# Sums of exponentials of two attention units folded to 64 partitions by DMA, with one product of ones for both

## The chip, the cores and the metric

The kernel runs on one core of one Trainium2 chip. The metric is the device time of that core in microseconds; before the change it is 3346.09 us, the median of three runs (3346.06 to 3346.24). In texts and profile lines PE is TensorE (PEld its weight loads), DVE is VectorE, ACT is ScalarE, POOL is GpSimd and SP is SyncE.

## What is computed

The reference is a chain of four layers on an image of two batches, 512 channels and 32 x 32 positions, all in float32. Layer 0 is a deformable attention with a learned position bias and an MLP, layer 1 a linear attention. Layers 2 and 3, which the change touches, are the same kind of layer: group norm, queries, keys and values for 8 heads of 64 channels, softmax attention over 1024 positions, a projection and the residual. Cut to what matters (layer 2):

```python
attn = jnp.einsum('bhcn,bhcm->bhnm', q, k) * scale
attn = jax.nn.softmax(attn, axis=-1)
out = jnp.einsum('bhnm,bhcm->bhcn', attn, v)
```

## The kernel before, in words

In layers 2 and 3 the method `attention` computes queries, keys and values, and then, where the logits are small enough for exponentials without a maximum, `heads_bounded` does the attention. Only that method is changed.

`heads_bounded` works through 16 units, one after the other. A unit is a batch b, a pair of heads p (two heads of 64 channels fill 128 partitions), and a half h of the 1024 queries (512 of them). Each unit has eight steps n, one for each block of 128 keys. In a step:

- `score` (L1509) forms the logits of both heads for these 128 keys: four products of 64 x 64 weights, one in each quadrant of TensorE, into a PSUM place of 128 x 1024. Two places, "a" and "b", take turns from step to step. ScalarE makes the exponentials e from it (L1513). So the score of a step needs the place that the exponential of two steps before has read.
- The exponentials of the eight steps are added up: those of steps 0, 1, 3, 5 on GpSimd in the tile `some` (L1518, L1520), those of 2, 4, 6, 7 on VectorE in the tile `sum` (L1523, L1525), and the two at the end of the unit (L1527). The tile `some` has a single buffer.
- `value` (L1538), two steps behind, multiplies the exponentials with the values, again in four quadrants; the result o collects over eight steps in the PSUM place "even" (h = 0) or "odd" (h = 1). The keys of one block lie on two halves of the partitions, and each half has its own sum in o: at the end ScalarE copies one (L1547) and VectorE adds the other (L1548).

Then the result has to be divided by the sums of exponentials. `divide` (L1550 on) multiplies `sum` with a matrix of ones, which adds over 64 partitions and spreads the sum over 64 rows at once: four products in four quadrants (L1555), into d in the PSUM place that o has just left. The two halves of the partitions give two partial sums: ScalarE copies the one (L1559), VectorE adds the other (L1560), takes the reciprocal (L1561) and multiplies the result with it (L1563). The bias of the values is put into a list and later added by ScalarE (L1567).

The order on TensorE, ScalarE, VectorE and GpSimd is written out by hand: within `manual_schedule` the instructions stand on each engine in the order in which the loop over i (128 steps and two more) issues them. In step i come `score(i)` with its exponential and additions, then, where i is a multiple of 8, a waiting bias, then `value(i - 2)`, then, where i % 8 is 4, `divide` of the unit before. From i = 78 on, every eighth step (i % 8 = 6) puts two additions for the projection on GpSimd (L1577, L812 on). The last unit's `divide` stands in the projection that follows. No scheduler moves any of it; semaphores are all that makes an engine wait.

Of the kernel before, what the change touches and what calls it, by code (L numbers as in the profile page):

```python
# [11 lines left out]
F32 = mybir.dt.float32  # L12
AF = mybir.ActivationFunctionType
ALU = mybir.AluOpType
# [4 lines left out]
P = 128  # L19
# [35 lines left out]
class Net:  # L55
# [1419 lines left out]
    def heads_bounded(self, k, ones, data, proj, out):  # L1475
# [7 lines left out]
        with ExitStack() as ctx:  # L1483
# [9 lines left out]
            def place(x, name):  # L1493
                return places[x].tile([P, 2, HF], F32, tag="o", name=name)
# [4 lines left out]
            def score(unit, n):  # L1499
                b, p, h, state = unit  # L1500
                qs, ks, _ = data[b]
                cut = slice(h * HF, (h + 1) * HF)

                at = {0: "b", 1: "a", 2: "odd"}.get(n) if unit is units[0] else None
                s = place(at or ("a", "b")[n % 2], f"s{k}{b}{p}{h}{n}")
                for par, rows in enumerate(halves):
                    for c in range(2):
                        at = n * P + c * DH
                        nc.tensor.matmul(  # L1509
                            s[halves[c], par, :], lhsT=ks[p][rows, at : at + DH], rhs=qs[p][rows, cut], start=True, stop=True  # L1510
                        )
                e = ep.tile([P, 2, HF], F32, tag="e", name=f"e{k}{b}{p}{h}{n}")
                nc.scalar.activation(e, s, AF.Exp, scale=DH**-0.5)  # L1513
                es = state.setdefault("e", {})
                es[n] = e
                if n == 1:
                    state["some"] = ap.tile([P, 2, HF], F32, tag="some", name=f"some{k}{b}{p}{h}")
                    nc.gpsimd.tensor_tensor(state["some"], es[0], e, ALU.add)  # L1518
                elif n in (3, 5):
                    nc.gpsimd.tensor_tensor(state["some"], state["some"], e, ALU.add)  # L1520
                elif n == 4:
                    state["sum"] = ap2.tile([P, 2, HF], F32, tag="sum", name=f"sum{k}{b}{p}{h}")
                    nc.vector.tensor_tensor(state["sum"], es[2], e, ALU.add)  # L1523
                elif n in (6, 7):
                    nc.vector.tensor_tensor(state["sum"], state["sum"], e, ALU.add)  # L1525
                if n == NB - 1:
                    nc.vector.tensor_tensor(state["sum"], state["sum"], state["some"], ALU.add)  # L1527

            def value(unit, n):
                b, p, h, state = unit  # L1530
                v = data[b][2]
                if n == 0:
                    state["o"] = place(home(h), f"o{k}{b}{p}{h}")
                o, e = state["o"], state["e"][n]
                for r, rows in enumerate(halves):
                    for par in range(2):
                        at = (2 * p + par) * DH
                        nc.tensor.matmul(  # L1538
                            o[halves[par], r, :],
                            lhsT=v[n // 2][rows, n % 2, at : at + DH],  # L1540
                            rhs=e[rows, par, :],
                            start=(n == 0),
                            stop=(n == NB - 1),
                        )
                if n == NB - 1:
                    res = data[b][0][p][:, h * HF : (h + 1) * HF]
                    nc.scalar.copy(res, o[:, 0, :])  # L1547
                    nc.vector.tensor_tensor(res, o[:, 1, :], res, ALU.add)  # L1548

            def divide(unit):  # L1550
                b, p, h, state = unit
# [47 lines left out]
            def project(b):  # L1599
                vec, pool = nc.vector, nc.gpsimd  # L1600

                def add(eng, p, i, what, biased=False):
                    o = 2 * (i // 2) + p
                    xt = self.xs[b][o][:, (i % 2) * HF : (i % 2 + 1) * HF]
                    if biased:
                        eng.scalar_tensor_tensor(xt, what, self.col(f"pb{k}", o), xt, ALU.add, ALU.add)
                    else:
                        eng.tensor_tensor(xt, xt, what, ALU.add)

                def store(p, i):  # L1610
                    o = 2 * (i // 2) + p
                    cut = slice((i % 2) * HF, (i % 2 + 1) * HF)
                    if out is not None:
                        nc.sync.dma_start(out[b, o][:, cut], self.xs[b][o][:, cut])

                us = ap2.tile([P, 2, HF], F32, tag="sum", name=f"pu{k}{b}")
                at = ("a", "b", "even", "a", "b", "even", "a") if b == 0 else ("odd", "even", "b", "odd", "even", "a", "b")
                for which, spot in zip(("P1", "P2", "P6", "P5", "P7", "P3", "P4"), at):
                    a, ri = SEVEN[which]
                    acc = place(spot, f"pb{k}{b}{which}")  # L1620
                    if out is not None and b == 1 and which == "P4":

                        for p, lo, hi, spot in ((0, 0, HF, None), (1, 0, HF // 2, "odd"), (1, HF // 2, HF, "even")):
                            piece = acc[:, 0, :] if spot is None else place(spot, f"pb{k}{lo}")[:, 0, lo:hi]
                            for c in range(2):
                                nc.tensor.matmul(
                                    piece,
                                    lhsT=left[a][:, c, p * P : (p + 1) * P],
                                    rhs=right[b][ri][c][:, lo:hi],
                                    start=c == 0,  # L1630
                                    stop=c == 1,
                                )
                            xt = self.xs[b][2 + p][:, lo:hi]
                            vec.scalar_tensor_tensor(xt, piece, self.col(f"pb{k}", 2 + p), xt, ALU.add, ALU.add)
                            nc.sync.dma_start(out[b, 2 + p][:, lo:hi], xt)
                        yield
                        continue
                    for p in range(2):
                        for c in range(2):
                            nc.tensor.matmul(  # L1640
                                acc[:, p, :],
                                lhsT=left[a][:, c, p * P : (p + 1) * P],
                                rhs=right[b][ri][c],
                                start=c == 0,
                                stop=c == 1,
                            )
                    for p in range(2):
                        got = acc[:, p, :]
                        u = us[:, p, :]
                        if which == "P1":  # L1650
                            nc.scalar.copy(u, got)
                            add(vec, p, 0, got, True)
                        elif which == "P2":
                            add(vec, p, 0, got)
                            store(p, 0)
                        elif which == "P6":
                            vec.tensor_tensor(u, got, u, ALU.add)
                        elif which == "P5":
                            add(vec, p, 1, got)
                            add(vec, p, 3, got)  # L1660
                        elif which == "P3":
                            add(vec, p, 1, got, True)
                            store(p, 1)
                        elif which == "P7":
                            add(vec, p, 3, got, True)
                            store(p, 3)
                            add(vec, p, 2, got)
                        else:
                            add(vec, p, 2, got, True)
                            store(p, 2)  # L1670
                    if which == "P6":
                        for i in (1, 3, 2):
                            for p in range(2):
                                add(pool, p, i, us[:, p, :])
                    yield
# [4 lines left out]
            with self.tc.manual_schedule(engines=engines):  # L1680
                for i in range(len(steps) + 2):
                    if i < len(steps):
                        score(*steps[i])
                    if i % NB == 0 and biases:
                        biases.pop(0)()
                    if i >= 2:
                        value(*steps[i - 2])
                    if i % NB == 4 and NB < i < len(steps):
                        divide(steps[i - NB][0])
                    if i % NB == 6 and i > len(steps) // 2 + NB:  # L1690
                        for _ in range(2):
                            sums.pop(0)()
# [236 lines left out]
```

## Time and profile before

| what | us |
|---|---|
| median of the runs (3) | 3346.09 |
| profiled execution, its span | 3346.7 |
| TensorE busy in it | 3336.4 |
| VectorE, ScalarE, GpSimd busy | 2313.9, 2056.6, 2178.0 |
| units of layer 2, stretch 2627 to 2860: TensorE busy | 233.00 of 233.00 |
| units of layer 3, stretch 3060 to 3293: TensorE busy | 233.00 of 233.00 |
| products of ones (L1555), one group of eight instructions | 1.04 from first start to last end |
| reciprocal of a unit (L1561) | 3.35 |

The profile is of one execution, and the span is the time from its first to its last instruction; the profile gives no other time for that execution. "Busy" is the time in which an engine works on at least one instruction. A float32 product is two instructions, so the four products of a group show as eight. Instructions of TensorE overlap: a group is seen for 1.04 us, while the next group begins earlier than that. In the lines of the timeline come start, duration, engine, line of the kernel, operation, what is written and read, the shape, and in brackets how long the engine had been idle and what ended that.

### The profile page before, as it was taken

How to read it: one execution, taken by the hardware profiler on the slowest of the kernel's cores; microseconds unless marked ns; L12 is line 12 of the kernel's file. 1: busy time of each engine (PE TensorE's matmuls, PEld its weight loads, DVE VectorE, ACT ScalarE, POOL GpSimd, SP SyncE). 2: the span in 40 equal slices, each digit the busy share in tenths (PEclk: the TensorE clock that was granted, in tenths of full speed). 3: DMA queues.
4: the chain of work that ended last, by engine and by line, in shares of the span. 5: the costliest groups of instructions: out<-in, count | busy, mean ns of one | idle time of the engine just before them, and what ended most of it. 6: DMA issues, size and time to landing. Idle time of an engine off the chain costs nothing.

```text
span 3346.7 us, 60378 instructions
## 1 busy us (share of the span) xinstructions
PE 3336.4 (100%) x25314; PEld 1242.0 (37%) x25314; DVE 2313.9 (69%) x2519; ACT 2056.6 (61%) x2171; POOL 2178.0 (65%) x1670
## 2 busy tenths in 40 slices
PE   9999999999999999999999999999999999999999
PEld 4333333333333333333333334444565533455333
DVE  6777777767766677777766665565565578755787
ACT  7887887888886688887888761111121466213662
POOL 6887878887877677878878874333323447634475
PEclk9999999999999999999999999999999999999999
DMA  6877877777877677877787862111000100000001
GB/s 178 160 159 151 162 157 156 159 157 156 161 154 141 123 157 146 165 154 156 159 173 159 162 139 99 42 46 38 1 1 1 38 2 1 14 0 14 1 1 52
DMA packets 102674, 342.68 MB, mean 102 GB/s; under 512 B 12656, under 2 KB 14832, under 8 KB 99312
## 3 DMA queue, kind: packets, MB, share of 16 engines
q0 software_dynamic: 73296, 266.90, 40.9%
q1 hardware_dynamic: 28080, 69.75, 7.2%
q8 instruction: 204, 3.34, 0.4%
q10 hardware_dynamic: 1008, 2.00, 0.2%
q14 instruction: 86, 0.70, 0.1%
HBM read 67.27 MB, written 4.46 MB: 21 GB/s over the span
## 4 chain that ended last, share of the span: by engine, by line
PE 97%; DVE 1%; POOL 1%; issue 1%; ACT 0%; DMA 0%; POOLq 0%; DVEq 0%; ACTq 0%
PE hp L664 52%; PE s L1509 7%; PE o L1538 7%; PE sim L696 3%; PE qk30P L1287 1%; PE qk20P L1287 1%; PE m_3P L842 1%; PE qk31P L1287 1%; PE m_7P L842 1%; PE m_5P L842 1%; PE m_2P L842 1%; PE m_0P L842 1%; PE qk21P L1287 1%; PE m_6P L842 1%; PE m_1P L842 1%; PE m_4P L842 1%
## 5 line engine op out<-in xcount | busy, mean ns | idle before, releaser
L664 PE MATMUL hp<-h,w 128*32 128x512 f32 x16384 | 1794.2, 593 | 0.3 <-ACT h L669 0.3
L633 DVE CUSTOM_DVE_ANT_1 h<-tx,bank 128x1024 f32<-128x1024 f32 (+1 forms) x1028 | 1180.6, 1211 | 309.1 <-PE hp L664 237.9
L669 ACT ACTIVATE h<-hp,magb 128x1024 f32<-128x1024 f32 x1024 | 1121.5, 1112 | 370.1 <-PE hp L664 362.5
L664 PEld LDWEIGHTS hp<-h,w 128*32 128x32 f32 x16384 | 525.8, 110 | 1200.6 <-issue 1146.9
L656 POOL DMA_DIRECT2D h<-h x509 | 451.4, 1021 | 363.1 <-ACT h L675 304.6
L682 POOL TENSOR_TENSOR h<-h,h 128x1024 f32<-128x1024 f32 x255 | 610.5, 2394 | 21.3
L680 POOL TENSOR_SCALAR h<-h,flip 128x1024 f32<-128x1024 f32 x256 | 447.0, 1746 | 1.0 <-ACT h L669 0.9
L1513 ACT ACTIVATE e<-s 128x1024 f32<-128x1024 f32 x256 | 262.0, 1025 | 155.3 <-PE s L1509 151.5
L671 ACT ACTIVATE h<-h,flip 128x1024 f32<-128x1024 f32 x256 | 291.5, 1138 | 0.0
L1509 PE MATMUL s<-q,k 64*64 64x512 f32 x2048 | 265.2, 589 | 0.0
L1538 PE MATMUL o<-e,v 64*64 64x512 f32 x2048 | 265.1, 589 | 0.0
L1520 POOL TENSOR_TENSOR some<-some,e 128x1024 f32<-128x1024 f32 x64 | 160.9, 2514 | 42.4 <-ACT e L1513 38.6
L1518 POOL TENSOR_TENSOR some<-e,e 128x1024 f32<-128x1024 f32 x32 | 75.8, 2368 | 157.8 <-DVE sum L1527 125.6
L673 POOL TENSOR_SCALAR h<-h,flip 128x1024 f32<-128x1024 f32 x128 | 143.4, 1120 | 43.7 <-ACT h L669 42.9
L675 ACT ACTIVATE h<-h,flip 128x1024 f32<-128x1024 f32 x128 | 145.6, 1138 | 0.0
L696 PE MATMUL sim<-h,ends 128*32 128x512 f32 x1024 | 133.3, 592 | 0.0
L1538 PEld LDWEIGHTS o<-e,v 64*64 64x64 f32 x2048 | 78.3, 133 | 141.4 <-issue 135.1
L1509 PEld LDWEIGHTS s<-q,k 64*64 64x64 f32 x2048 | 78.1, 133 | 141.0 <-issue 115.5
L1523 DVE TENSOR_TENSOR sum<-e,e 128x1024 f32<-128x1024 f32 x32 | 57.3, 1792 | 99.9 <-ACT e L1513 99.9
L812 POOL TENSOR_TENSOR mlp_w<-mlp_w 128x512 f32<-128x512 f32 x16 | 21.3, 1332 | 158.5 <-DMA mlp_w<-in_mlp_w 152.7
L903 ACT ACTIVATE mh<-mh,cols 128x512 f32<-128x512 f32 x64 | 46.1, 721 | 124.3 <-DVE mh L921 65.4
L1561 DVE RECIPROCAL r<-r 128x512 f32<-128x512 f32 x32 | 107.3, 3353 | 1.1
(549 smaller groups left out, 3321.0 us busy)
## 6 DMA issues: line engine op xcount, KB each, us to landing
h<-h POOLq DMA_DIRECT2D x509, 512.0 KB, 6.4
lb<-logs SPq DMA_DIRECT2D x63, 512.0 KB, 5.3
mlp_w<-in_mlp_w SPq DMA_DIRECT2D x16, 1024.0 KB, 4.8
x<-in_x SPq DMA_DIRECT2D x8, 512.0 KB, 8.1
qkw<-in_l_qk SPq DMA_DIRECT2D x2, 2048.0 KB, 8.3
out<-x SPq DMA_DIRECT2D x15, 256.0 KB, 2.1
vw<-in_l_v SPq DMA_DIRECT2D x2, 1024.0 KB, 7.9
projw<-in_l_proj SPq DMA_DIRECT2D x2, 1024.0 KB, 4.7
```

The costliest lines, as they stand in the source:

```text
L633: self.nc.vector._custom_dve(TENSOR_ADD_SAT, out=h1[r][:, k, cut, :], in0=x[:, jj, 2 * r + k, :].unsqueeze(1).to_broadcast([P, H // parts, ...
L656: nc.gpsimd.dma_start(to, what, accum_op=ALU.add)
L664: nc.tensor.matmul(hp[rows, cut], lhsT=self.l0w2[:, 32 * q : 32 * q + 32], rhs=h1[k][:, cut], start=True, stop=True)
L669: nc.scalar.activation(y, hp, AF.Relu, bias=self.magb[:, q : q + 1])
L671: nc.scalar.activation(ys[0], ys[0], AF.Copy, scale=self.flip[:, 0:1])
L680: nc.gpsimd.tensor_scalar(y, y, self.flip[:, 2:3], 1.0, ALU.mult, ALU.mult)
L682: (nc.vector if final else nc.gpsimd).tensor_tensor(y, y, ys[2], ALU.add)
L696: nc.tensor.matmul(sims[u][at : at + 32, :], lhsT=self.ends[:, 28 - 4 * o : 60 - 4 * o], rhs=z[jj][:, h * HF : (h + 1) * HF], start=(o == ...
L842: self.nc.tensor.matmul(acc[p], lhsT=w[:, a, k, p * P : (p + 1) * P], rhs=right(r, k), start=k == 0, stop=k == 1)
L1509: nc.tensor.matmul(s[halves[c], par, :], lhsT=ks[p][rows, at : at + DH], rhs=qs[p][rows, cut], start=True, stop=True)
L1513: nc.scalar.activation(e, s, AF.Exp, scale=DH**-0.5)
L1538: nc.tensor.matmul(o[halves[par], r, :], lhsT=v[n // 2][rows, n % 2, at : at + DH], rhs=e[rows, par, :], start=(n == 0), stop=(n == NB - 1),)
```

## The change

For every unit but the last two, one half of `sum` is added to the other half by a DMA transfer that GpSimd issues, from 64 partitions to the 64 others (unit h = 0 ends on partitions 0 to 63, h = 1 on 64 to 127). Two units, which are the two query halves of one b and p, then share a single group of four products of ones: each unit's folded half takes two of the quadrants, and d holds the finished sums of both. ScalarE copies all of d (128 x 1024) into the second unit's `sum` tile, VectorE takes the reciprocal of each unit's half from there and multiplies. The shared product stands at step 6 of the unit after the pair, the first unit's reciprocal and multiplication right behind it, the second unit's at step 1 of the next unit. Biases can be issued every fourth step instead of every eighth. The tag `sum` gets three buffers instead of two. The last two units keep `divide`.

```diff
-                    state["sum"] = ap2.tile([P, 2, HF], F32, tag="sum", name=f"sum{k}{b}{p}{h}")
+                    state["sum"] = ap2.tile([P, 2, HF], F32, tag="sum", bufs=3, name=f"sum{k}{b}{p}{h}")
...
+            def fold(unit):
+                b, p, h, state = unit
+                to, of = halves[h], halves[1 - h]
+                nc.gpsimd.dma_start(state["sum"][to, :, :], state["sum"][of, :, :], accum_op=ALU.add)
+
+            def divide_two(both):
+                b, p, _, _ = both[0]
+                d = place("odd", f"d{k}{b}{p}")
+                for par in range(2):
+                    for rows, (_, _, h, state) in zip(halves, both):
+                        nc.tensor.matmul(
+                            d[halves[par], h, :], lhsT=ones[rows, :], rhs=state["sum"][rows, par, :], start=True, stop=True
+                        )
+                t = both[1][3]["sum"]
+                nc.scalar.copy(t, d)
+                for h in range(2):
+                    nc.vector.reciprocal(t[:, h, :], t[:, h, :])
+                    res = data[b][0][p][:, h * HF : (h + 1) * HF]
+                    nc.vector.tensor_tensor(res, res, t[:, h, :], ALU.mult)
+                    biases.append(lambda res=res: nc.scalar.activation(res, res, AF.Identity, bias=self.col(f"vb{k}", p)))
+                    yield
...
-                us = ap2.tile([P, 2, HF], F32, tag="sum", name=f"pu{k}{b}")
+                us = ap2.tile([P, 2, HF], F32, tag="sum", bufs=3, name=f"pu{k}{b}")
...
-                    if i % NB == 0 and biases:
+                    if i % 4 == 0 and biases:
                         biases.pop(0)()
                     if i >= 2:
                         value(*steps[i - 2])
-                    if i % NB == 4 and NB < i < len(steps):
-                        divide(steps[i - NB][0])
+                    done, at = divmod(i, NB)
+                    if at == 0 and 0 < done < len(units) - 1:
+                        fold(units[done - 1])
+                    if at == 6 and done % 2 == 0 and 0 < done < len(units):
+                        divided = divide_two(units[done - 2 : done])
+                        next(divided)
+                    if at == 1 and done % 2 == 1 and 1 < done < len(units):
+                        next(divided)
+                    if at == 4 and done == len(units) - 1:
+                        divide(units[-2])
```

In the changed kernel the fold stands in line 1553, the shared product in 1560, the wide copy in 1564, the reciprocals in 1566, the multiplications in 1568 and the biases in 1569. NB is 8, HF 512 and DH 64.

## The prediction

> **What bounds the kernel now.** I read the page first (busy time, chain), then the windows of the two attention stages, then the timeline of one unit, then the groups that the change touches.
>
> ```profile
> PE 3336.4 (100%) x25314; PEld 1242.0 (37%) x25314; DVE 2313.9 (69%) x2519; ACT 2056.6 (61%) x2171; POOL 2178.0 (65%) x1670
> ...
> PE 97%; DVE 1%; POOL 1%; issue 1%; ACT 0%; DMA 0%; POOLq 0%; DVEq 0%; ACTq 0%
> ```
>
> ```profile
> 2627.00:2860.00 233.00, 233.00 (x2167) 83.04 (x2160) 175.84 (x122) 156.62 (x174) 141.78 (x62) 1.00 0.02 6
> 3060.00:3293.00 233.00, 233.00 (x2167) 83.08 (x2160) 176.11 (x122) 156.66 (x174) 141.73 (x62) 1.00 0.02 6
> ```
>
> The columns of the last two lines are TensorE, weight loads, VectorE, ScalarE, GpSimd. In the sixteen units of a layer TensorE never stops: 233.00 of 233.00 us. So a product taken out there is worth its whole length, and a wait put in front of one costs its whole length. Nothing else is near full, but ScalarE and VectorE work in a fixed order, and that order is what I follow below.
>
> One unit in the timeline (start, duration, engine, line), first on VectorE, then on ScalarE, then on GpSimd:
>
> ```profile
> 2661.68 1.92 DVE L1523 TENSOR_TENSOR sum<-e,e 128x1024 f32<-128x1024 f32 x1 [3.58 <-ACT e L1513]
> 2663.53 0.68 DVE L1560 TENSOR_TENSOR r<-d,r 128x512 f32<-128x512 f32 x1
> 2664.24 3.35 DVE L1561 RECIPROCAL r<-r 128x512 f32<-128x512 f32 x1
> 2667.62 0.69 DVE L1563 TENSOR_TENSOR q<-q,r 128x512 f32<-128x512 f32 x1
> ```
>
> ```profile
> 2668.38 1.02 ACT L1513 ACTIVATE e<-s 128x1024 f32<-128x1024 f32 x1 [0.66 <-PE s L1509]
> 2669.30 0.71 ACT L1567 ACTIVATE q<-q,cols 128x512 f32<-128x512 f32 x1
> 2670.15 1.03 ACT L1513 ACTIVATE e<-s 128x1024 f32<-128x1024 f32 x1
> ```
>
> ```profile
> 2660.16 2.36 POOL L1520 TENSOR_TENSOR some<-some,e 128x1024 f32<-128x1024 f32 x1
> 2664.37 2.37 POOL L1520 TENSOR_TENSOR some<-some,e 128x1024 f32<-128x1024 f32 x1 [1.84 <-ACT e L1513]
> 2672.26 2.37 POOL L1518 TENSOR_TENSOR some<-e,e 128x1024 f32<-128x1024 f32 x1 [5.52 <-DVE sum L1527]
> ```
>
> Two things are to be seen. First the pitch: d starts at 2661.24 and again at 2675.83, 14.59 us for 17 groups of products (8 scores, 8 values, 1 d), so one group takes 0.858 us and one step (score and value) 1.716. Second the slack: d's reciprocal and multiplication are over at 2668.31, and the bias that reads them comes a microsecond later, behind the exponential of 2668.38. It waits for nothing.
>
> [...] L1523 takes 1.92 us where it starts 0.84 us before a GpSimd add (2660.16 to 2662.52) ends, and 1.23 alone; over all 32 it is 1224/1898/3203 ns. [...] the rows above keep their written order. [...] d, s and o all show 8 instructions of 589 ns in 1.04 us. The DMA's price comes from the trace.
>
> **What the change removes.** Per layer, fourteen products of ones (one per unit) become seven (one per pair); units 14 and 15 keep their own. Seven groups of 0.858 us, two layers: 14 x 0.858 = 12.0 us of TensorE, all on the path. VectorE loses 14 PSUM additions (0.68 us) per layer and ScalarE one copy in two; both have room, so that is worth nothing by itself. The quadrants stay four, but the half of the rows now changes with every product, in scores and values with every second one. No row shows that order; its cost lies between nothing and the loss of one half of the overlap, 0.86 us a pair, and I take nothing, since the four quadrants are still four different ones.
>
> **What it adds: the folds.** Fourteen GpSimd transfers of 256 KB per layer. Nearest rows:
>
> ```profile
> L656 POOL DMA_DIRECT2D h<-h x509: 850/888/1217, 30.4 to 1988.8; - x170
> ...
> DMA to landing us min/median/max: 4.4/6.4/12.3
> ```
>
> These are 512 KB accumulations in a stage where queue 0 is crowded; here it is empty, so I take 4.5 us (bounds 3 to 7). The fold waits for L1527, the end of a unit's sum, and behind it on GpSimd stands the next unit's first addition L1518, which waits for L1527 anyway (5.52 us idle above). It starts about 0.6 us later (at 501.38 an operation follows two such issues of 500.20). The second fold of a pair is the close one: its unit's last exponential ends about 19 us after the previous d, VectorE's three additions behind it [...] about 23, and the next d stands at about 30: 7 us for 4.5. Hidden; what a fold takes beyond 7 us is TensorE's, in every pair.
>
> **What it moves: the biases.** Here I expect the cost. Before, d stands at step 4 and its bias at step 0 of the next unit, four steps later. Now call a pair A, B and the next one C, D. d stands after step 6 of C, A's bias behind the exponential of D0 (two steps later), B's bias behind that of D4, and B's reciprocal only at D1. A bias that waits for VectorE holds every later exponential on ScalarE, and score D3 needs the score place that exponential D1 frees, D7 that of D5. Times from the start of d:
>
> 1. Bias A. C6's sum (L1525) waits for GpSimd's third addition (exponential C5 ends at -1.3, the addition runs from -1.15 to 1.2) and ends at 2.3; the wide copy of d is done by 2.15. Reciprocal 2.3 to 5.65, multiplication to 6.37, bias at 6.4. Exponential D1 could have started at 5.4 (score at 4.29; an exponential starts 1.11 after its score's first product).
> 2. How fast ScalarE goes on is seen where a bias waits already:
>
> ```profile
> 2785.08 1.02 ACT L1513 ACTIVATE e<-s 128x1024 f32<-128x1024 f32 x1 [0.60 <-PE s L1509]
> 2786.89 0.72 ACT L1567 ACTIVATE q<-q,cols 128x512 f32<-128x512 f32 x1 [0.78 <-DVE q L1563]
> 2787.52 1.00 ACT L1513 ACTIVATE e<-s 128x1024 f32<-128x1024 f32 x1
> ```
>
> The exponential follows 0.63 us after the bias: 7.03 to 8.05. Score D3 is due at 9 x 0.858 = 7.72 and starts about 0.05 after the exponential (a weight load follows an ACT end by that elsewhere): late by 0.4 us.
> 3. Bias B. VectorE goes on: C7's sum 6.3 to 7.6, L1527 7.6 to 8.9, L1548 from 8.8, reciprocal B 9.5 to 12.9. GpSimd: fold at 9.0, L1518 9.6 to 12.0, L1520 from 12.1 to 14.4 (starts 2.49 apart). Multiplication B [...] ends at 15.0. Bias B at 15.05, exponential D5 15.7 to 16.7. Score D7 is due at 17 x 0.858 + 0.4 = 14.98: late by 1.8 us.
> 4. A pair: 0.4 + 1.8 - 0.86 = +1.34 us. Four pairs per layer are so: 5.4.
> 5. In the last three pairs GpSimd makes two more half-size additions per unit (L1577, L812 on), between its third addition and the fold. Multiplication A meets one, as L1563 does there today (691/1045/1227 ns); I take 0.6 us more, +1.94 for two pairs. The last pair's bias B has unit 14's own d in front of score D7, 0.86 us of cover: +1.04. Together 4.9.
>
> Sum: 2 x (5.4 + 4.9) = +20.6 us. Against the profiled span, 3346.7 + 20.6 = 3367.3; the span stands 0.6 us above the median, so 3367 us. The third buffer and project's sums I cost at nothing: with three, A's buffer is asked for again six steps (10 us) after d reads it, and B's 9 us after multiplication B.
>
> **Rivals.**
> - *Only the late biases.* If multiplication B misses GpSimd's turn, it ends at 13.6, and if C6's sum misses it too, all is 0.15 us earlier: D7 is late by about 0.4, D3 by 0.27, a pair gains 0.19: 14 x -0.19 = -2.6 us, 3343. For it: 0.8 us decide, and a slower issue of the fold than 0.6 us would put the addition behind. Against: rows of up to 3203 ns for L1523.
> - *The clean saving* (the other side): D1 and D5 start in time and 12.0 us go, 3334. Its place is ScalarE behind D0 and D4. Bias A has to start by 6.0 and B by 12.9, so the reciprocals 0.4 us and[...] 2.2 us earlier than worked out. For it: ScalarE is busy only 156.62 of 233 us. Against: the busy share says nothing about an order.
> - *Late folds.* At 9 us to landing d itself waits, 2 us in some twelve of the fourteen pairs: 24 us more, 3391. Against: the queue is empty (DMA share 0.02).
> - *The product does not do its work in four quadrants at once*: up to 14 x 0.86 = 12 us more, 3379.
>
> **How the numbers follow.** Bias [...] 0.58 (own range 3356 to 3380); only the late biases 0.15; clean saving 0.09; late folds 0.10; a slower product or some smaller wait in between 0.08. A measurement tells 0.2%, 6.7 us, from nothing. Faster: the clean saving and a good end of the first rival, 0.12. Within: the rest of that rival and half of the in-between, 0.15. Slower 0.73. The range reaches to the first rival below and into the late folds above, 3341 to 3385, and leaves out the clean saving and the worst folds.
>
> **What would show it.** Right: 18 groups of products of ones instead of 32; gaps on TensorE before scores, released by the exponential (L1513); the bias (L1569) idle before until DVE's multiplication (L1568), and that one with a median near 2 us rather than 0.69; windows of 233 us grown to about 243. Wrong: no idle before biases (the clean saving), multiplications of 0.7 us (only the late biases), or d waiting for a DMA (late folds).

## The result, and the profile after

The changed kernel takes 3385.43 us (median of 4 runs, 3385.02 to 3386.12); the kernel before, run beside it, 3346.11 (4 runs). The ratio is 1.0117, 95% interval 1.0105 to 1.0129: 39.3 us slower, where 20.6 was forecast.

The page of the changed kernel, busy times and the chain that ended last:

```profile
PE 3337.0 (99%) x25202; PEld 1236.2 (37%) x25202; DVE 2342.7 (69%) x2491; ACT 2047.0 (61%) x2157; POOL 2201.8 (65%) x1698
...
PE 90%; DVE 6%; issue 2%; ACT 1%; POOL 1%; DMA 0%; ACTq 0%; DVEq 0%; POOLq 0%
```

TensorE has 112 instructions less and is busy as long as before, and 6% of the chain is now VectorE's. The place is the two attention stages. In the stretches that were 233.00 of 233.00 us before (columns: TensorE, weight loads, VectorE, ScalarE, GpSimd, then TensorE's clock), it is

```profile
2627.00:2860.00 233.00, 216.89 (x1948) 75.17 (x1944) 172.50 (x97) 139.67 (x152) 144.23 (x70) 0.98 0.10 18
3060.00:3293.00 233.00, 217.00 (x1886) 82.36 (x1884) 167.92 (x106) 131.67 (x145) 129.55 (x64) 0.99 0.11 20
```

16 us of standing in each, and a clock of 0.98 and 0.99. From the first score to the last value product of a layer, the starts in the trace give 232.25 us before in both layers, and 252.42 and 251.26 after: 39.2 us more, which is the whole loss.

The waits of the changed kernel, 2600 to 2900 us (total, times, longest):

```profile
ACT q L1569 <- DVE q L1568: 38.5, 14, 3.6
...
PE s L1509 <- ACT e L1513: 17.3, 12, 2.1
```

All fourteen biases of the layer wait for their multiplication, and scores wait for exponentials. (How long a score is late I take from the distance between the starts of products, 0.858 us from group to group where nothing is late; this view counts only the time in which TensorE shows nothing at all.) The second pair of layer 2 in the timeline shows how one wait leads to the other, with the names of the prediction: A and B are the pair, C and D the two units after it, D3 is step 3 of D. The shared product d starts at 2692.21:

```profile
2689.22 2.68 DVE L1523 TENSOR_TENSOR sum<-e,e 128x1024 f32<-128x1024 f32 x1 [3.90 <-ACT e L1513]
...
2691.07 3.06 POOL L1520 TENSOR_TENSOR some<-some,e 128x1024 f32<-128x1024 f32 x1 [0.26 <-ACT e L1513]
...
2692.21 1.04 PE L1560 MATMUL d<-sum,ones 64*64 64x512 f32 x8
...
2692.71 2.50 DVE L1525 TENSOR_TENSOR sum<-sum,e 128x1024 f32<-128x1024 f32 x1 [0.81 <-ACT e L1513]
...
2698.51 0.69 DVE L1568 TENSOR_TENSOR q<-q,sum 128x512 f32<-128x512 f32 x1
...
2699.24 0.72 ACT L1569 ACTIVATE q<-q,cols 128x512 f32<-128x512 f32 x1 [2.32 <-DVE q L1568]
2699.86 1.01 ACT L1513 ACTIVATE e<-s 128x1024 f32<-128x1024 f32 x1
...
2700.92 1.09 PE L1509 MATMUL s<-q,k 64*64 64x512 f32 x8 [0.81 <-ACT e L1513]
...
2702.18 3.34 DVE L1566 RECIPROCAL sum<-sum 128x512 f32<-128x512 f32 x1
2702.20 0.82 POOL L1553 DMA_DIRECT2D sum<-sum  x1 [8.07 <-PE s L1509]
...
2705.50 2.35 POOL L1520 TENSOR_TENSOR some<-some,e 128x1024 f32<-128x1024 f32 x1
2705.56 2.84 DVE L1568 TENSOR_TENSOR q<-q,sum 128x512 f32<-128x512 f32 x1
...
2708.44 0.72 ACT L1569 ACTIVATE q<-q,cols 128x512 f32<-128x512 f32 x1 [3.56 <-DVE q L1568]
2709.07 1.92 ACT L1513 ACTIVATE e<-s 128x1024 f32<-128x1024 f32 x2
...
2710.12 1.09 PE L1509 MATMUL s<-q,k 64*64 64x512 f32 x8 [2.10 <-ACT e L1513]
...
2712.39 1.95 PE L1509 MATMUL s<-q,k 64*64 64x512 f32 x8
```

Read it down: bias A waits 2.32 us for its multiplication, the exponential behind it frees its place late, score D3 is late by 0.99 us. Multiplication B takes 2.84 us where A's took 0.69: GpSimd's addition (L1520, 2705.50 to 2707.85) began 0.06 us ahead of it, and it ends 0.55 us after that. I call this a meeting: a VectorE operation and a GpSimd addition under way at once, of which the later takes longer. Bias B waits 3.56 us and score D7 is 2.28 us late. The last line is a new thing: a score whose eight instructions take 1.95 us instead of 1.04. The granted clock is 0.50 there, from 2711.4 to 2714.8.

Over both layers the distances between products give waits before D3 of 0.3 to 1.2 us (together 10.5) and before D7 of mostly 2.0 to 2.3, once 3.4 and less in the last pairs (together 30.4). Five stretches of 3.41 us have a clock of 0.50, 1.7 us lost in each: 8.5. With the products saved, -12.0 + 10.5 + 30.4 + 8.5 = +37.4 of the 39.2 us; the rest is many small gaps, which I did not allot.

The folds, their transfers, and what waited for them:

```profile
L1553 POOL DMA_DIRECT2D sum<-sum x28: 812/823/867, 2639.3 to 3302.2; - x28
...
  PEld d L1560: 0.2, 1
...
DMA to landing us min/median/max: 3.4/3.4/5.5
```

The shared product waited for a fold once, for 0.2 us. So late landings are not the cause.

### The profile page after: what moved, and what is told of

It is laid out like the page before. It is cut to its first block, busy times and chain, and to the rows that moved or that the text cites. A ratio compares the mean times of both kernels' runs of the same rounds, so it can differ in the third digit from the quotient of the medians.

```text
span 3383.2 us, 60250 instructions
## 1 busy us (share of the span) xinstructions
PE 3337.0 (99%) x25202; PEld 1236.2 (37%) x25202; DVE 2342.7 (69%) x2491; ACT 2047.0 (61%) x2157; POOL 2201.8 (65%) x1698
## 4 chain that ended last, share of the span: by engine, by line
PE 90%; DVE 6%; issue 2%; ACT 1%; POOL 1%; DMA 0%; ACTq 0%; DVEq 0%; POOLq 0%
PE hp L664 51%; PE s L1509 4%; PE o L1538 4%; PE sim L696 3%; DVE sum L1566 3%; PE qk30P L1287 1%; PE qk20P L1287 1%; PE qk31P L1287 1%; PE m_7P L842 1%; PE m_4P L842 1%; PE m_3P L842 1%; PE m_2P L842 1%; PE m_0P L842 1%; PE qk21P L1287 1%; PE m_6P L842 1%
## 5 line engine op out<-in xcount | busy, mean ns | idle before, releaser
L1509 PE MATMUL s<-q,k 64*64 64x512 f32 x2048 | 272.6, 601 | 35.9 <-ACT e L1513 35.5
L1520 POOL TENSOR_TENSOR some<-some,e 128x1024 f32<-128x1024 f32 x64 | 161.6, 2525 | 50.8 <-ACT e L1513 48.6
L1525 DVE TENSOR_TENSOR sum<-sum,e 128x1024 f32<-128x1024 f32 x64 | 120.8, 1887 | 41.9 <-ACT e L1513 40.0
L1553 POOL DMA_DIRECT2D sum<-sum x28 | 23.1, 827 | 131.4 <-PE s L1509 96.6
L1523 DVE TENSOR_TENSOR sum<-e,e 128x1024 f32<-128x1024 f32 x32 | 57.5, 1796 | 70.6 <-ACT e L1513 70.6
```

The source lines that it names most:

```text
L1509: nc.tensor.matmul(s[halves[c], par, :], lhsT=ks[p][rows, at : at + DH], rhs=qs[p][rows, cut], start=True, stop=True)
```

## The experiments

My theory was now that the order of the biases is the cause: a bias that waits for VectorE holds the exponentials behind it, B's far longer than it must because its multiplication meets GpSimd's addition (2.84 us for 0.69). The rivals: the folds cost time of themselves, by their landing or by what they hold up on GpSimd; or the shared product costs more than it seems to. In all of the experiments the kernel before ran beside them, at 3346.1 to 3346.3 us.

**Biases later.** Bias A six steps after d instead of two, bias B eleven instead of six, nothing else changed:

```diff
...
-                    if i % 4 == 0 and biases:
+                    if (i % 16 in (12, 1) or i >= len(steps)) and biases:
```

> The changed kernel with its biases later on ScalarE: A's behind the exponential of D4, six steps after d (was two), B's eleven steps after d (was six); everything else as in the change. Theory 1 (a bias that waits for VectorE holds the exponentials behind it, TensorE waits for these, and after some of these waits its clock is halved for 3.4 us): no wait of TensorE for an exponential is left, no halved clock in the two attention stages, and the clean saving of 14 groups appears: 3346.1 - 12.0 = 3334 us, 3332 to 3339. Rival 2 (the folds cost the time, by their landing or by what they hold up on GpSimd): about 3385, since the folds stay. Rival 3 (the shared product itself is slower than a group of four): 3334 plus what it loses, above 3346.

Measured: 3353.20 us, ratio 1.0020 (1.0013 to 1.0028). 32 us of the loss went with the order of one list, so the mechanism holds; but the rest of the theory fell: 3353 is 19 us above the clean saving. In the first four pairs of a layer 0.3 us a pair is left at most; in the later ones waits up to 2.86 us stay, and one stretch of half clock. One of those waits in the timeline:

```profile
2791.74 5.11 POOL L1520 TENSOR_TENSOR some<-some,e 128x1024 f32<-128x1024 f32 x2
2791.80 2.85 DVE L1568 TENSOR_TENSOR q<-q,sum 128x512 f32<-128x512 f32 x1
...
2794.57 3.37 DVE L1523 TENSOR_TENSOR sum<-e,e 128x1024 f32<-128x1024 f32 x1
...
2798.03 1.94 ACT L1513 ACTIVATE e<-s 128x1024 f32<-128x1024 f32 x2 [4.40 <-DVE sum L1523]
...
2799.11 1.09 PE L1509 MATMUL s<-q,k 64*64 64x512 f32 x8 [2.67 <-ACT e L1513]
```

No bias is in it. Twice in a row a VectorE operation begins while an addition of GpSimd is under way, and takes longer (2.85 instead of 0.69 us, 3.37 instead of 1.2), and the exponential waits until the second of the two has read its buffer e (4.40 us). A second bottleneck lay behind the first.

**Biases at other steps.** Bias A four steps after d, B eight:

```diff
-                    if i % 4 == 0 and biases:
+                    if i % 4 == 2 and biases:
```

> The same with a smaller delay: A's bias four steps after d, B's eight. Theory 1: A's multiplication ends 6.3 to 7.0 us after d, the exponential in front of the bias at 8.1, so A does not wait; B's ends at 14.6 to 15.2 and the exponential in front at 15.0, so B waits for 0.2 us or less and TensorE for nothing or little: 3334 to 3341. Rivals 2 and 3: 3385 and above 3346, as with the longer delay.

Measured: 3353.17 us, 1.0020 (1.0013 to 1.0028), the same as with the later ones: at most 0.3 us per pair in the first half, in the second 0.23, 1.83 and 0.97 in each of two pairs, and 1.2 before unit 14's own d. Between these two places it doesn't matter where exactly the biases stand; what is left isn't theirs.

**Only bias B later.** Bias A stays two steps after d:

```diff
-                    if i % 4 == 0 and biases:
+                    if (i % 16 in (8, 1) or i >= len(steps)) and biases:
```

> The changed kernel with B's bias eleven steps after d and A's left two steps after it. It parts the two biases. Theory 1: what is left over e1 (3353.2) is A's waits before score D3, 0.3 to 1.2 us in fourteen pairs (10.5 us in the changed kernel, part of which e1 has elsewhere): 3357 to 3364, and no halved clock but after a wait of more than 2 us. If B's bias is not the larger part: 3370 or more. From the six kernels so far I also expect the clock: every stretch of 3.41 us, counted from one halved stretch to the next, in which TensorE stands for more than about 2.05 us is followed by a halved one, and no other is.

Measured: 3353.95 us, 1.0025 (1.0015 to 1.0034), below what I expected. Bias A alone costs 0.28 to 0.31 us in each of the first four pairs, and no more than the runs above had there for other reasons; later waits of up to 2.1 us before D3 take the place of those that the runs above had a few steps on. So moving B's bias alone takes away nearly all of the 32 us, and in the first four pairs the waits of 1 us before D3 in the changed kernel, 0.3 here, are in good part an echo of B's.

**A waiting bias alone.** The kernel before, without folds or shared products; only the bias stands two steps earlier, behind the exponential two steps after d:

```diff
-                    if i % NB == 0 and biases:
+                    if (i % NB == 6 or i >= len(steps)) and biases:
```

> The kernel before with each bias two steps after its d instead of four (behind the exponential of step 6). No folds, no shared product. Theory 1: the multiplication ends 7.1 us after d begins, the exponential of step 6 at 4.8, so ScalarE stands for 2.3 us; the exponential of step 7 is late by 2.3 minus its slack, 1.1 us on TensorE in each of 30 units: 33 us, and up to 8 more for halved clocks: 3379 to 3388. Rivals 2 and 3: 3346, as neither their folds nor their product is in it.

Measured: 3387.36 us, 1.0122 (1.0105 to 1.0139), 41.1 us more. Scores wait 1.05 to 1.30 us per unit, once 1.57, where 1.1 was worked out; together 32.6 us. A further 2.1 us stand before the last value product of each layer. The waits of one layer, 2620 to 2880 us:

```profile
ACT q L1567 <- DVE q L1563: 36.4, 15, 2.6
...
PE s L1509 <- ACT e L1513: 13.7, 14, 1.1
```

The mechanism is shown by itself: one bias placed too early in each unit costs this kernel as much as the whole change cost, without fold or shared product.

**The addition beside multiplication B.** The changed kernel without GpSimd's addition of step 3 in the odd units (these sums lack one of eight exponentials), so that no addition is under way at multiplication B. GpSimd has 2.4 us less to do in each of these units, too:

```diff
+                elif n == 3 and h == 1:
+                    pass
                 elif n in (3, 5):
```

> The changed kernel without GpSimd's addition of step 3 in the second unit of each pair (the exponentials of that block of keys are left out of that unit's sum, so the kernel computes something else); the biases stay where the change has them. Theory 1a (multiplication B stands behind this addition [...], and that makes the long wait of 2.0 to 2.3 us before score D7, which also halves the clock): multiplication B falls from some 2.85 to 0.7 us, the wait before D7 to 0.4 us, the halved clocks go: 3385.4 - 13 x 1.8 - 8.5 = 3353, 3349 to 3358. Theory 1b (the bias is late because the reciprocal is[...]): 3380 to 3385.

Measured: 3351.80 us, 1.0017 (1.0010 to 1.0023). The multiplications:

```profile
L1570 DVE TENSOR_TENSOR q<-q,sum x28: 691/692/720, 2667.4 to 3289.1; 128x512 f32<-128x512 f32 x28
```

In the changed kernel the same row (L1568 there) reads 691/1600/2859. Biases stand where the change put them, and 33.6 us are gone, the halved clocks too. So the early bias and this meeting make the loss together: with late biases the kernel is 6.9 us above the kernel before, without this addition 5.6.

**Folds alone.** The kernel before with the same transfers, added into a tile that nothing reads:

```diff
...
+                nc.gpsimd.dma_start(aside[to, :, :], state["sum"][of, :, :], accum_op=ALU.add)
...
+                    if i % NB == 0 and 0 < i // NB < len(units) - 1:
+                        fold(units[i // NB - 1])
```

> The kernel before with the folds added and nothing else: 14 per layer, each adding half of a finished sum into a tile that nothing reads. Theory 1: hidden behind GpSimd's slack, 3346, at most 2 us more. Rival 2: the part of the 39 us that the folds cost shows here, above 3352 if they are the cause. Rival 3: 3346.

Measured: 3354.55 us, 1.0023 (1.0013 to 1.0033). That is 8.3 us, more than I expected: the rival had a part of it after all. No product is late for the first eleven units of a layer, but for the next four d waits about 1.0 us each, 8 us in both layers. In the timeline:

```profile
2789.87 0.83 POOL L1556 DMA_DIRECT2D aside<-sum  x1 [2.71 <-DVE sum L1527]
...
2790.26 1.05 PE L1563 MATMUL d<-sum,ones 64*64 64x512 f32 x8
2790.44 2.66 POOL L1518 TENSOR_TENSOR some<-e,e 128x1024 f32<-128x1024 f32 x1
...
2790.73 3.46 DVE L1523 TENSOR_TENSOR sum<-e,e 128x1024 f32<-128x1024 f32 x1 [0.56 <-ACT e L1513]
...
2805.11 0.68 DVE L1548 TENSOR_TENSOR q<-o,q 128x512 f32<-128x512 f32 x1
...
2805.85 1.09 PE L1563 MATMUL d<-sum,ones 64*64 64x512 f32 x8 [0.80 <-DVE q L1548]
```

and the two additions in the kernel before, a unit later:

```profile
2805.39 2.37 POOL L1518 TENSOR_TENSOR some<-e,e 128x1024 f32<-128x1024 f32 x1 [2.56 <-DVE sum L1527]
...
2807.63 1.23 DVE L1523 TENSOR_TENSOR sum<-e,e 128x1024 f32<-128x1024 f32 x1 [1.78 <-ACT e L1513]
```

No one waits for the transfer. But without folds L1518 starts 2.24 us ahead of VectorE's L1523, which then takes 1.23 us; with them it starts 0.29 us ahead, and L1523 takes 3.46. Of this shift 0.57 us is the issue itself (2789.87 to 2790.44); the rest is an L1527 that came later, and where that began I did not follow. VectorE is late for the rest of the unit, L1548 empties the place of o late, and d needs that place.

**The price of a product.** The kernel before with the four products of ones formed once more, in fourteen places:

```diff
+                if h == 1 and unit is not units[-1]:
+                    for r, rows in enumerate(halves):
+                        for par in range(2):
+                            nc.tensor.matmul(
+                                d[halves[par], r, :], lhsT=ones[rows, :], rhs=state["sum"][rows, par, :], start=True, stop=True
+                            )
```

> The kernel before, with the product of ones done twice in every second unit (7 a layer, 14 groups of four more, into the same place). It prices one group: theory 1 takes 0.858 us for each, all on the path: 3346.3 + 12.0 = 3358.3, 3357 to 3360. If part of a group were hidden, the clean saving would be less than 12.0 and the sum here smaller.

Measured: 3358.06 us, 1.0035 (1.0022 to 1.0048): +11.9, or 0.85 us per group. The saving of 12.0 us is real. The order of the quadrants here is that of `divide`; that a shared product isn't dearer shows in the changed kernel, where the next group starts 0.86 us after each of its fourteen shared d.

**Half of the change.** If the second half of a layer has no room for meetings of VectorE and GpSimd, the change should be made in the first half alone: folds and shared products for the first eight units, `divide` as before for the other eight, late biases:

```diff
...
-                    if at == 0 and 0 < done < len(units) - 1:
+                    if at == 0 and 0 < done <= 8:
                         fold(units[done - 1])
-                    if at == 6 and done % 2 == 0 and 0 < done < len(units):
+                    if at == 6 and done % 2 == 0 and 0 < done <= 8:
...
-                    if at == 4 and done == len(units) - 1:
-                        divide(units[-2])
+                    if at == 4 and 8 < done < len(units):
+                        divide(units[done - 1])
```

> Folds and shared products only for the first four pairs of a layer, with biases six and eleven steps after d; from unit 8 on everything as before the change. Theory 2 (what is left in the runs with late biases, 19 us above the clean saving, comes from the second half of each layer, where GpSimd has its additions for the projection [...]): 8 groups saved are 6.9 us, waits of 0.3 us in six or seven pairs cost 2: 3346.3 - 4.9 = 3341.4, 3339 to 3344, faster than both kernels. If the folds cost by themselves wherever they stand: 3346 or more.

Measured: 3341.22 us, 0.9985 (0.9979 to 0.9992), faster than both kernels. The stretches of the two attention stages:

```profile
2627.00:2860.00 233.00, 232.74 (x2138) 82.75 (x2131) 190.82 (x115) 155.24 (x171) 158.59 (x70) 1.00 0.07 15
3060.00:3293.00 233.00, 232.78 (x2120) 83.02 (x2113) 193.32 (x118) 152.98 (x169) 158.13 (x70) 1.00 0.06 11
```

TensorE is full again but for 0.3 us in each, and has 8 x 0.858 = 6.9 us less to do. Four waits of 0.3 us over both layers give 1.2 of it back; 5.0 us were gained.

**All folds, with the second division moved.** Reciprocal and multiplication B go behind the first of VectorE's sums of D (step 4), the biases go as late as in the first run, B's one step more, and GpSimd's projection additions are put together:

```diff
...
-                    if at == 1 and done % 2 == 1 and 1 < done < len(units):
+                    if at == 4 and done % 2 == 1 and 1 < done < len(units):
                         next(divided)
...
-                    if i % NB == 6 and i > len(steps) // 2 + NB:
-                        for _ in range(2):
+                    if i % 16 == 6 and i > len(steps) // 2:
+                        for _ in range(4 if i < 118 else 2):
                             sums.pop(0)()
```

> All folds and shared products, but the second unit's reciprocal and multiplication stand behind the addition of step 4 (L1523) instead of in front of it, its bias at step 2 of the unit after, the first unit's bias at step 4; and GpSimd's additions for the projection stand four together where VectorE has a reciprocal, instead of two in every unit. Theory 2 (exponentials wait because VectorE's additions, pushed back by reciprocal B [...], hold the six buffers of exponentials): most waits go, 3334 to 3342. If [...]: waits of 2 to 3 us per pair stay in three pairs of each layer, 3346 to 3354.

Measured: 3345.27 us, 0.9998 (0.9989 to 1.0006): no difference to the kernel before, between the two expectations. The first three pairs of each layer have no wait left and the fourth one of 0.35 us; the second half keeps 1.6, 1.6 and 1.0 us, and behind each attention stage some 0.7 us more go. The second half has two half-size GpSimd additions more per unit. A sum over the traces suggests that VectorE and GpSimd have no room left there. In the meetings of the changed kernel's two attention stages the later operation ends after the earlier one, in the median, by 1.08 us for VectorE's sums (64 meetings; 1.22 us alone), 0.55 for its multiplications (17; 0.69 alone), 2.23 for L1520 (21; 2.36 alone) and 1.13 for GpSimd's half-size additions (11; 1.27 alone). So I let their times add up. By the shortest distance from one start to the next, GpSimd has six additions of 2.31 us and four of 1.24 in a pair, VectorE eight of 1.14 and two of 0.61, some 29.2 us. A pair lasts 28.3 us after the change (33 groups of 0.858) and 29.2 before it (34 groups), where the same operations made TensorE wait for nothing. This sum is an estimate from those distances, not a measurement of how full the two are. Whether another order would avoid the waits was not tried.

**Half of it, with the second division moved.** The half version with step 4 instead of 1 and B's bias one step on:

```diff
...
-                    if at == 1 and done % 2 == 1 and 1 < done <= 9:
+                    if at == 4 and done % 2 == 1 and 1 < done <= 9:
```

> The two versions that helped put together: folds and shared products in the first four pairs of a layer alone, with the second unit's reciprocal and multiplication behind the addition of step 4 and the biases six and twelve steps after d; from unit 8 on as before the change. Theory 2: the waits of 0.3 us that the first four pairs still showed go, as they did in the first half of e8, and all of 8 x 0.858 = 6.9 us is kept: 3346.2 - 6.9 = 3339.3, 3338 to 3341. If those waits come from the folds themselves: 3341, as in e7.

Measured: 3342.73 us, 0.9990 (0.9983 to 0.9996). The waits of 0.3 us went, as expected, but at the seam, before the first product of ones that is a unit's own again, stands one of some 1.5 us in each layer. I laid it to the fourth second division, and put that one alone back to step 1:

```diff
-                    if at == 4 and done % 2 == 1 and 1 < done <= 9:
+                    if at == (4 if done < 9 else 1) and done % 2 == 1 and 1 < done <= 9:
```

> Shared products in the first four pairs of each layer, as in the two runs with half of the folds: the first three second reciprocals behind the sum of D's first exponentials (step 4 of D), the fourth, next to the units that keep their own product, back at step 1 as in the first of those runs. If the wait of 1.54 us at the seam in the run before came from that fourth reciprocal, it goes, and the two waits of 0.3 us per layer that the first of those runs had do not come back in the first three pairs: 3346.2 - 8 x 0.858 = 3339.3, up to 3340 with one small wait left at the fourth pair of each layer. If instead the seam costs the same wherever that reciprocal stands, the time is again 3342.7.

Measured: 3342.23 us, 0.9987 (0.9981 to 0.9994), and the wait is still there, 1.3 to 1.4 us. So it was not that. The timeline of this kernel:

```profile
2762.93 2.55 POOL L1520 TENSOR_TENSOR some<-some,e 128x1024 f32<-128x1024 f32 x1 [0.22 <-ACT e L1513]
2763.18 3.38 DVE L1523 TENSOR_TENSOR sum<-e,e 128x1024 f32<-128x1024 f32 x1
...
2774.99 0.68 DVE L1548 TENSOR_TENSOR q<-o,q 128x512 f32<-128x512 f32 x1
...
2775.72 1.09 PE L1577 MATMUL d<-sum,ones 64*64 64x512 f32 x8 [1.18 <-DVE q L1548]
```

and that of the first half version at the same work:

```profile
2763.58 1.21 DVE L1523 TENSOR_TENSOR sum<-e,e 128x1024 f32<-128x1024 f32 x1
2763.66 3.36 POOL L1520 TENSOR_TENSOR some<-some,e 128x1024 f32<-128x1024 f32 x1 [0.55 <-ACT e L1513]
```

It is the kind of wait that the folds alone had: L1523 begins 0.25 us after GpSimd's addition, takes 3.38 us, and L1548 and d are late. In the first half version TensorE had lost 0.6 us before, GpSimd got its exponential later, and VectorE was first by 0.08 us. So, as the two traces have it, taking small waits away let the two meet in the wrong order; no run was made to show that. The first half version stays the best measured, though these three lie within each other's intervals.

## Why the prediction was wrong in size

The path and the waits were right; the sum was too small. Two terms failed most: the slower clock after a wait, for which the sum had nothing (measured 8.5 us), and the wait of bias B (some 23.4 us forecast, 30.4 measured).

- **The saving, -12.0.** Right: 0.85 us per group by experiment. The order of the quadrants costs nothing: the group before d and the group after it are 0.86 us from it, as before the change.
- **The mechanism and the sign.** Right: late biases hold ScalarE, D3 and D7 wait, multiplication B meets GpSimd's addition (2.84 us). Either half taken away takes 32 to 34 us away.
- **Steps 1 and 2 (bias A, 0.4 us).** Right for A alone, 0.3 us by experiment. In the changed kernel it is often 1 us: L1525 was put at 2.3 us after d, but ends at 3.0, because L1520 before it, which began while L1523 was under way (2689.22 to 2691.90), took 3.06 us instead of 2.36 and ran to 1.9 rather than 1.2. I followed one meeting, and not the one that delays the next. With the 0.6 us for the last three pairs, the steps gave A 9.2 us in all; it is 10.5.
- **Step 3 (bias B, 1.8 us).** Mis-sized: mostly 2.28, in all 30.4 us for some 23.4. The fold was issued 10.0 us after d instead of 9.0, L1520 so began at 13.3 instead of 12.1 and the multiplication behind it ended at 16.2 instead of 15.0; score D7 was due only 0.6 later for A's wait.
- **No step: the clock.** The prediction has it that a wait costs its whole length, and no more. But five waits before D7 were followed by a stretch at a clock of 0.50; these stretches, 8.5 us, are not in the sum. With A (1.3) and B (7.0) they make 16.8 of the 18.7 us between forecast and result.
- **"It takes nothing beyond 7 us, so it is hidden" (the folds).** The landing of 3.4 us is hidden, as I took it to be with 4.5. But I asked only who waits for the transfer. The folds also move GpSimd's additions against VectorE's, and that costs 8.3 us in the kernel before; what it is in the changed kernel was not measured apart.
- **The rivals.** *The clean saving* rested on the biases alone; with them out of the way the kernel still stood at 3353, not 3334. *Only the late biases* gave 3343; with the addition beside multiplication B left out it is 3352. *Late folds* and *a slower product* are refuted, by the 0.2 us and by the distance of 0.86 us behind each d.
- **The base.** I set the span of 3346.7 beside the median of 3346.1. The later runs list both, and a run's time is 1.8 us above its span; typical spans of the kernel before are 3344.4. So the execution I read was 2.3 us longer than usual. It has a stretch at a clock of 0.51 between layers 1 and 2 (2444.1 to 2447.5) that the profile of the changed kernel lacks. As a base for the sum the median was right. (In step 5, 1.94 - 0.86 is 1.08, not 1.04; that is 0.1 us over both layers.)

## What to carry to other kernels

A consumer issued in order belongs behind its producer by the producer's worst case, meetings with another engine included (multiplication B took 2.84 us for 0.69); when it is early, everything behind it pays, so ask first where a moved instruction stands and only then what it costs. A wait taken away shows the next one: test a fix against the clean saving, and where one stage has no room left, make the change only in the part that has. An operation that nobody waits for isn't free if it shifts which of two others begins first (8.3 us for the folds alone).

## What the runs showed of the hardware

- TensorE's clock was 0.50 five times in the attention stages of the changed kernel, for 3.413 us each, and the starts of these stretches lie 28, 10, 104 and 19 times 3.413 us apart. I counted in windows on this grid. Each of the five windows in which TensorE stood 2.2 us or more in all (up to 2.7) was followed by one at 0.50; none of the others, with up to 2.06 us, was. (Standing time is what the distance between starts has over 0.429 us, at which TensorE's instructions start four at a time when nothing is late.) I had expected a limit of about 2.05 us before the run with B's bias alone moved, and that run had a window of 2.066 with a clock of 1.00 in the next; whether there is a limit between this and 2.2 us these windows do not show. Three windows of the changed kernel, the columns as above:

```profile
2708.00:2711.40 3.40, 1.30 (x15) 0.51 (x16) 1.92 (x3) 2.58 (x4) 1.19 (x1) 1.00 0.00 0
2711.40:2714.80 3.40, 3.40 (x20) 1.07 (x16) 3.30 (x2) 1.38 (x2) 1.17 (x1) 0.50 0.00 0
2714.80:2718.20 3.40, 3.40 (x36) 1.23 (x32) 1.59 (x3) 2.15 (x4) 1.35 (x2) 1.00 0.00 0
```

  A clock of 0.50 in the second, with 20 instructions instead of 36. Such a stretch costs 1.7 us on top of the wait; five of the fourteen waits before D7 in the changed kernel were followed by one.
- In a meeting of two additions, the one that began first was the fast one, by over 2 us: L1523 took 1.21 us when it began 0.08 us ahead of GpSimd's L1520, and 3.38 us when it began 0.25 us behind (the first half version and the last).
- An adding transfer of 256 KB from 64 partitions to 64 lands 3.4 us after its issue in the median (5.5 at most); the issue takes GpSimd 0.82 us.
